# Attention scores from two float32r parts, two 64-row matmuls side by side in the array

## The chip, the cores and the metric

The kernel runs on one core of one Trainium2 chip. The metric is the device time of one execution in microseconds; the shown figure is the median of several executions. The core's engines are PE (TensorE, matrix products), DVE (VectorE), ACT (ScalarE), POOL (GpSimd) and SP (SyncE, which here only issues transfers). In the profile, PEld is the weight load of PE, which can run beside a matmul.

## The reference, cut to what matters

The input `x` is 16 batches of 512 positions of 128 numbers. Six layers are applied one after the other, each added to `x`:

```python
x = x + 0.5 * _L0_ffn_ref(_layernorm(x), ...)     # "kan"
x = x + _L0_attn_ref(_layernorm(x), ...)          # attention
x = x + 0.5 * _L0_ffn_ref(_layernorm(x), ...)     # "kan" again
x = x + 0.5 * _L1_ffn_ref(_layernorm(x), ...)     # experts
x = x + _L1_attn_ref(_layernorm(x), ...)          # a recurrence
x = x + 0.5 * _L1_ffn_ref(_layernorm(x), ...)     # experts again
```

The change lies in the attention. It has 16 query heads of 8 dimensions; 4 query heads share one key and value head; queries and keys are rotated by position (`rope`):

```python
att = jnp.einsum('bhqd,bhkd->bhqk', q, k) * scale
att = jnp.where(causal, att, jnp.finfo(att.dtype).min)
att = jax.nn.softmax(att, axis=-1)
y = jnp.einsum('bhqk,bhkd->bhqd', att, v)
```

Everything is float32.

## The kernel before, in words

**Two stages.** The attention stage goes through the 16 batches in order. Behind it the experts' stage does the three last layers. The order of the instructions on every engine is written out by hand: a batch's loop (called a row below) has 44 turns (`TURNS`), 11 banks of scores for each of the 4 key heads `r`. In each turn the main work is written down first (one bank of `weights` of batch b, one bank of `maxima` of batch b+1), and then `turn()` lets every side generator (outputs, the two kans, the projection of a later batch, the routing) write down one step, as far as the turn's budget `MOST` of each engine allows. An engine executes its instructions in that order.

**Scores twice.** A score tile of one key head and one block of 128 positions is computed twice. `maxima` (line 612) has 128 queries on the output's rows and keys along it; DVE masks it and takes the maximum over the keys (lines 617 and 622). The wider banks are masked on PE first (line 608). `weights` (line 675) has 128 keys on the rows and queries along it; ACT takes the exponential (line 678) and POOL zeroes what lies above the diagonal (line 680). The maximum of each query is subtracted within the score matmul: it is one more contraction row, against a row of ones. A head group's 11 banks hold 16 matmuls, four each of 512, 384, 256 and 128 columns, in `maxima` and in `weights` alike.

**Operands.** PE multiplies bf16 here, so that float32 queries and keys are cut into three bf16 parts (`parts`, lines 394 to 407: a copy on ACT and three subtractions on POOL, for queries and for keys), written to DRAM and read back as 9 products of parts: 72 contraction rows (`spread`, lines 477 and 485). `max_rows` cuts the maxima into three parts, turns them on PE, and brings them by way of DRAM into rows 96 to 98 of the query tile (lines 626 to 653). So `maxima` contracts over 72 rows and `weights` over 99. Ten query tiles `QP` and three key tiles `KP` go round; a query tile is read by `maxima` in one row and by `weights` in the next.

**Outputs.** `outputs` (lines 686 to 723) multiplies the weights by the values: 32 output rows for each of the 4 query heads of a group, the fourth of the array's columns for each (line 698). Eight of each 32 rows are values and one the sum. ACT copies (line 703), PE turns 4 blocks (line 711), DVE divides (lines 715 and 716), once for each `r`.

**Score banks.** PSUM has two banks for `maxima` (`scp`) and two for `weights` (`stp`).

**Experts.** Their weights are loaded at the start of the last batch's row, all at once, into query and key tiles that are free by then (lines 829 to 839).

Of the kernel before, what the change touches and what calls it, by code (L numbers as in the profile page):

```python
# [8 lines left out]
F32 = mybir.dt.float32  # L9
# [8 lines left out]
P = 128  # L18
# [11 lines left out]
NQP = 10  # L30
NKP = 3
MXR = 96
# [16 lines left out]
def tile_macaron(  # L49
# [51 lines left out]
    with ExitStack() as ph:  # L101
# [54 lines left out]
        nc.scalar.dma_start(out=gate_sb, in_=gate_in)  # L156
        rbias = cst.tile([P, 2, NV], F32, name="rbias")

        w2d = cst.tile([P, 2, NV, MH], F32, name="w2d")
        eye4 = cst.tile([P, MH], F32, name="eye4")  # L160
# [6 lines left out]
        KR = NR * HD  # L167
        wq = cst.tile([D, NH, HD], F32, name="wq")
        nc.sync.dma_start(out=wq, in_=wq_in.rearrange("k (h d) -> k h d", d=HD))
        wk = cst.tile([D, 2, NR, HD], F32, name="wk")  # L170
        nc.sync.dma_start(out=wk[:, 0, :, :], in_=wk_in.rearrange("k (h d) -> k h d", d=HD))
# [3 lines left out]
        nc.sync.dma_start(out=wo, in_=wo_in)  # L175
# [3 lines left out]
        for b in range(1, B):  # L179
            load(b)  # L180
        hh = HD // 2
        wqr = cst.tile([D, NH, HD], F32, name="wqr")
        identb = cst.tile([P, P], BF16, name="identb")
# [3 lines left out]

        QP = [qkp.tile([P, NG, S], BF16, name=f"qp{i}", tag=f"qp{i}") for i in range(NQP)]
        KP = [qkp.tile([P, NR, S], BF16, name=f"kp{i}", tag=f"kp{i}") for i in range(NKP)]
        ROWS = slice(0, MXR + 3)  # L190

        def packed(b):
            return [QP[(NR * b + r) % NQP] for r in range(NR)], KP[b % NKP]

# [199 lines left out]
        def parts(r, dst, copies, **work):  # L394

            yield from need(**work)
            copies(dst[:, 0, :], r)
            yield
            yield from need(pool=1.15)
            nc.gpsimd.tensor_tensor(dst[:, 1, :], r, dst[:, 0, :], ALU.subtract)  # L400
            yield
            yield from need(pool=1.15)
            nc.gpsimd.tensor_tensor(r, r, dst[:, 0, :], ALU.subtract)
            yield
            yield from need(pool=1.3)
            nc.gpsimd.tensor_tensor(dst[:, 2, :], r, dst[:, 1, :], ALU.subtract)
            yield

        def spread(part, heads, name):

            scr = tc.dram_tile([3, HD, heads, S], BF16, name=name)
            for i in range(3):
                nc.sync.dma_start(out=scr[i].rearrange("d h t -> h d t"), in_=part[:, i, :])
            return scr

        def attn_in(b, st):
            _, xT = yield from norm(x[b])
            ka = w1p.tile([KR, S], F32, name="rope_ka")
            kb = w1p.tile([KR, S], F32, name="rope_kb")
            ta = w1p.tile([P, S], F32, name="rope_a")  # L420
            tb = w1p.tile([P, S], F32, name="rope_b")
            qpart = w1p.tile([P, 3, S], BF16, name="qpart")
            kpart = w1p.tile([KR, 3, S], BF16, name="kpart")
# [12 lines left out]
            pk = yield from bank([2 * KR, S], F32, "ps_pk", 0.9)  # L436
            nc.tensor.matmul(pk, lhsT=wk.rearrange("k w h d -> k (w h d)"), rhs=xT, start=True, stop=True)
            later.append(lambda: nc.vector.tensor_mul(ka, pk[0:KR, :], rope[0:KR, 0, :]))
# [3 lines left out]
            take(dve=0.7)  # L442
            pv = yield from bank([P, NT, KR], F32, "ps_v", 0.9)
            for c in range(NT):
                nc.tensor.matmul(pv[:, c, :], lhsT=xT[:, bass.ts(c, P)], rhs=wv, start=True, stop=True)
            later.append(lambda: nc.vector.tensor_mul(kb, pk[KR : 2 * KR, :], rope[KR : 2 * KR, 1, :]))
            yield
            take(dve=0.7)
            freed()
            qp_steps = parts(ta, qpart, nc.scalar.copy, act=0.6)  # L450
# [3 lines left out]
            nc.gpsimd.memset(va[:, :, :, HD:32], 0.0)  # L454
            nc.gpsimd.memset(va[:, :, :, HD : HD + 1], 1.0)
            later.append(lambda: nc.vector.tensor_copy(va[:, :, :, 0:HD], pv.rearrange("p c (r d) -> p c r d", d=HD)))
            yield
            take(dve=0.3)
# [3 lines left out]
            def keys():  # L462
                yield from need(pool=1.25)
                nc.gpsimd.tensor_tensor(ka, ka, kb, ALU.add)
                yield
                yield
                yield
                yield from parts(ka, kpart, nc.scalar.copy, act=0.6)

            yield from together(qp_steps, keys())  # L470
            qp, kp = packed(b)

            ks = spread(kpart, NR, f"ks{b}")
            qs = spread(qpart, NH, f"qs{b}")
            N = 3 * HD
            for j in range(3):
                nc.sync.dma_start(
                    out=kp[j * N : (j + 1) * N, :, :],
                    in_=ks[j].rearrange("d r t -> d (r t)").unsqueeze(0).to_broadcast([3, HD, NR * S]),
                )  # L480
            for r in range(NR):
                while taken[0] < NR * b + r - NQP + 1:
                    yield
                src = qs[:, :, r * NG : (r + 1) * NG, :].rearrange("i d h t -> (i d) (h t)")
                nc.sync.dma_start(out=qp[r][0 : 3 * N, :, :],
                                  in_=src.unsqueeze(0).to_broadcast([3, N, NG * S]))
            yield

        def centered(ps, w):

            ps = ps[:, 0 : w.shape[1]]
            nc.tensor.matmul(ps, lhsT=center, rhs=w, start=True, stop=True)
            nc.vector.tensor_copy(w, ps)
# [6 lines left out]
        def cleared(pack):  # L500

            nc.vector.memset(pack[MXR - 32 : MXR, :, :], 0.0)

        def keys_cleared(i):

            cleared(KP[i])
            nc.vector.memset(KP[i][MXR : MXR + 3, :, :], 1.0)

        def prepare():
# [26 lines left out]
            centered(psc[:, 1, :], wk[:, 0, :, :].rearrange("k h d -> k (h d)"))  # L536
# [5 lines left out]
            nc.vector.tensor_copy(wk[:, 1, :, 0:hh], wk[:, 0, :, hh:HD])  # L542
            nc.vector.tensor_copy(wk[:, 1, :, hh:HD], wk[:, 0, :, 0:hh])
# [5 lines left out]
            make_identity(nc, identb)  # L549
            nc.gpsimd.memset(causal[:, 0 : S - P], 0.0)  # L550
            make_causal_mask(nc, own, NEG)
            for i in range(1, NR):
                cleared(QP[i])
                yield
            for _ in range(16):
                yield
            for i in range(NR, NQP):
                if i - NR < NKP - 1:
                    keys_cleared(i - NR + 1)
                yield  # L560
                yield
                cleared(QP[i])
                yield
                yield
# [33 lines left out]
        def maxima(b, st):  # L598
            qp, kp = packed(b)
            for half in range(2):  # L600
                maxs = w2p.tile([P, NT, NH // 2], F32, name="maxs")
                for r in (2 * half, 2 * half + 1):
                    for c, gs in BANKS:
# [3 lines left out]
                        if not alone:  # L607
                            nc.tensor.matmul(v[:, :, n - P : n], lhsT=identb,
                                             rhs=own.unsqueeze(1).to_broadcast([P, len(gs), P]),
                                             start=True, stop=False, skip_group_check=True)  # L610
# [642 lines left out]
```

## Time and profile before

| | us |
|---|---|
| median of 3 executions (range) | 1645.51 (1640.77 to 1647.1) |
| the profiled execution | 1638.15 |
| its span | 1636.4 |
| first score matmul of `maxima` starts at | 68.1 |
| first score matmul of `weights` starts at (row of batch 0) | 118.5 |
| rows of batches 3 to 8, each | 53.9 |
| rows of batches 9 to 12 | 54.9, 57.0, 55.3, 55.1 |
| rows of batches 0, 1, 2, 13, 14, 15 | 44.1, 49.6, 55.2, 48.7, 48.2, 38.5 |
| last score matmul of `weights` ends at | 948.2 |

The profiled execution's own time holds its span and 1.75 us around it. A row is counted from its first matmul on line 675 to that of the next. Durations of single instructions are given in us or ns; a matmul's duration in the profile is longer than the time in which PE can start the next one, so that what PE needs for a stream of matmuls is read from their starts.

### The profile page before, as it was taken

Reading aid. Unit: us, or ns where it says so; the run is one execution under the profiler, and the core shown is the slowest. Engines: PE = TensorE matmul, PEld = TensorE weight load, DVE = VectorE, ACT = ScalarE, POOL = GpSimd, SP = SyncE. Lnnn points to the kernel's source line nnn. Section 1 sums busy time; section 2 is a strip of 40 time slices with the busy share of each in tenths; the row PEclk is TensorE's granted clock in tenths of the full one; section 3 lists DMA queues with packets and bytes.
Section 4 is the critical chain, followed back from the end, with each engine's and each line's share of the span. In section 5 each row is a group of like instructions: output and inputs, shape, how many; then the busy total and the mean of one; then the engine's idle time right before and its main releaser. Section 6 shows DMA issues by size and latency. Waiting matters only on the chain.

```text
span 1636.4 us, 33218 instructions
## 1 busy us (share of the span) xinstructions
PE 1527.1 (93%) x11881; PEld 1062.5 (65%) x11881; DVE 1173.9 (72%) x3646; ACT 988.6 (60%) x1884; POOL 977.5 (60%) x1455
## 2 busy tenths in 40 slices
PE   5689999999999999999998899999998999999998
PEld 2234444454445444445444479999997999999998
DVE  6578878888888888888898345975579755873343
ACT  3336677877778777777766865444443444444443
POOL 2634566566655664665564666667665566756673
PEclk9779999999999999999999999999999999999999
DMA  5110110111011100110122113223322223323332
GB/s 128 64 69 24 55 54 26 42 55 53 32 40 52 57 25 36 57 47 29 42 71 69 51 44 69 59 54 72 72 68 56 66 62 72 78 51 74 67 67 58
DMA packets 99290, 92.74 MB, mean 57 GB/s; under 512 B 13245, under 2 KB 87686, under 8 KB 98886
## 3 DMA queue, kind: packets, MB, share of 16 engines
q1 hardware_dynamic: 76732, 67.72, 13.4%
q0 software_dynamic: 21584, 22.89, 7.7%
q8 instruction: 93, 1.52, 0.4%
q14 instruction: 71, 0.58, 0.1%
q10 hardware_dynamic: 810, 0.02, 0.0%
HBM read 59.07 MB, written 35.45 MB: 58 GB/s over the span
## 4 chain that ended last, share of the span: by engine, by line
PE 70%; DVE 20%; ACT 4%; issue 3%; POOL 2%; DMA 1%; SPq 0%; DVEq 0%; POOLq 0%; ACTq 0%
PE ps_h L967 12%; PE ps_y L980 12%; PE ps_av L698 7%; PE ps_st L675 6%; PE ps_sc L612 6%; DVE below L617 5%; PE acc L931 4%; PE ps_kg L366 3%; PE ps_s L339 3%; PE ps_t L319 3%; DVE ln_st L288 2%; ACT pt L678 2%; PE ps_ko L387 2%; DVE wk L801 2%; DVE tok L799 1%
## 5 line engine op out<-in xcount | busy, mean ns | idle before, releaser
L680 POOL TENSOR_SCALAR_AFFINE_SELECT pt<-pt 128x128 f32<-128x128 f32 (+2 forms) x704 | 253.2, 367 | 326.3 <-ACT pt L678 321.2
L678 ACT ACTIVATE pt<-ps_st 128x512 f32<-128x512 f32 x682 | 368.0, 563 | 94.5 <-PE ps_st L675 89.0
L617 DVE CUSTOM_DVE_ANT_0 below<-ps_sc,causal 128x512 bf16<-128x512 f32 (+1 forms) x512 | 315.2, 616 | 79.8 <-PE ps_sc L612 64.5
L870 POOL DMA_INDIRECT xg<-xnd,tokI x256 | 254.4, 994 | 86.7 <-issue 38.3
L969 ACT ACTIVATE mo<-ps_h 128x512 f32<-128x512 f32 x256 | 152.8, 597 | 228.1 <-PE ps_h L967 227.2
L967 PE MATMUL ps_h<-xin,mw 128*128 128x128 f32 x2048 | 273.8, 277 | 0.0
L980 PE MATMUL ps_y<-mw,mo 128*128 128x128 f32 x2048 | 272.0, 276 | 0.0
L612 PE MATMUL ps_sc<-kp,qp 72*128 72x512 bf16 (+3 forms) x1024 | 258.9, 304 | 12.6 <-DVE maxs L617 7.6
L675 PE MATMUL ps_st<-qp,kp 99*128 99x512 bf16 x992 | 249.9, 303 | 16.7 <-ACT pt L678 16.2
L967 PEld LDWEIGHTS ps_h<-xin,mw 128*128 128x128 f32 x2048 | 251.8, 193 | 12.8 <-issue 10.8
L980 PEld LDWEIGHTS ps_y<-mw,mo 128*128 128x128 f32 x2048 | 250.8, 193 | 0.1
L675 PEld LDWEIGHTS <-kp 99*128 99x128 bf16 x1024 | 94.4, 100 | 175.9 <-issue 158.4
L372 ACT ACTIVATE kan_h<-kan_s,rbias,kw 128x512 f32<-128x512 f32 x256 | 205.6, 812 | 4.1 <-PE ps_kg L366 4.1
L997 POOL DMA_INDIRECT sum<-mo,tokI x93 | 151.4, 1628 | 75.7 <-ACT mo L969 16.6
L698 PE MATMUL ps_av<-pt,va 128*32 128x512 f32 (+3 forms) x2048 | 165.2, 440 | 0.0
L622 DVE TENSOR_REDUCE maxs<-ps_sc 128x2 f32<-128x512 f32 (+1 forms) x192 | 130.1, 685 | 35.0 <-PE ps_sc L612 34.5
L612 PEld LDWEIGHTS <-qp 72*128 72x128 bf16 x1024 | 96.0, 99 | 80.4 <-issue 58.0
L698 PEld LDWEIGHTS ps_av<-pt,va 128*32 128x32 f32 x2048 | 53.5, 109 | 93.6 <-issue 42.5
L295 POOL TENSOR_TENSOR ln_rstd<-ln_rstd,mhalf 128x4 f32<-128x4 f32 x96 | 102.7, 1069 | 8.0
L294 POOL TENSOR_SCALAR ln_rstd<-ln_mv 128x4 f32<-128x4 f32 x96 | 22.0, 229 | 119.6 <-DVE ln_mv L292 119.4
L319 PE MATMUL ps_t<-ident,kan_x 128*128 128x128 f32 x384 | 63.5, 289 | 30.8 <-DVE kan_x L309 21.4
L986 DVE SCALAR_TENSOR_TENSOR ye<-ps_y,gainT,ye 128x128 fp32r<-128x128 f32 x83 | 28.8, 347 | 83.4 <-ACT ye L983 83.1
(196 smaller groups left out, 2487.5 us busy)
## 6 DMA issues: line engine op xcount, KB each, us to landing
qp<-qs SPq DMA_DIRECT2D x64, 288.0 KB
xnd<-kan_x SPq DMA_DIRECT2D x32, 256.0 KB
sum<-x SPq DMA_DIRECT2D x62, 128.0 KB
qs<-qpart SPq DMA_DIRECT2D x48, 128.0 KB
kp<-ks SPq DMA_DIRECT2D x48, 96.0 KB
x<-in_L_attn_x_dram SPq DMA_DIRECT2D x16, 256.0 KB
mw<-in_L_ffn_w_dram SPq DMA_DIRECT2D x16, 256.0 KB
xg<-xnd,tokI POOLq DMA_INDIRECT x256, 2.6
```

Source lines behind the costliest of these rows:

```text
L372: nc.scalar.activation(h, sk[half], AF.Relu, bias=rbias[:, half, v : v + 1], scale=kw1[:, half, v : v + 1])
L612: nc.tensor.matmul(v[:, u, 0:n], lhsT=qp[r][0 : 9 * HD, g, bass.ts(c, P)], rhs=kp[0 : 9 * HD, r, 0:n], start=alone, stop=(u == len(gs) - 1 ...
L617: nc.vector.tensor_tensor_reduce(below[:, 0:n], v[:, 0, 0:n], causal[:, S - n : S], 1.0, LOWEST, ALU.add, ALU.max, accum_out=maxs[:, c, h ...
L675: nc.tensor.matmul(v[:, u, 0:n], lhsT=kp[ROWS, r, bass.ts(c, P)], rhs=qp[r][ROWS, g, c * P : S], start=True, stop=True)
L678: nc.scalar.activation(o, v[:, :, 0:n], AF.Exp, scale=HD ** -0.5)
L680: nc.gpsimd.affine_select(out=dg, in_=dg, compare_op=ALU.is_ge, fill=0.0, base=0, pattern=[[0, len(gs)], [1, P]], channel_multiplier=-1)
L698: nc.tensor.matmul(po[32 * g : 32 * g + 32, c * P : S], lhsT=va[:, c, r, :], rhs=pt[:, g, OFF[c] : OFF[c] + n], start=(c == 0), stop=(c == ...
L870: nc.gpsimd.indirect_dma_start(out=xgs[i // E % 2][:, i % E, :], out_offset=None, in_=xnd[b], in_offset=bass.IndirectOffsetOnAxis(ap=tokI[ ...
L967: nc.tensor.matmul(pst[:, f, :], lhsT=mw1[e][:, bass.ts(f, P)], rhs=xins[i // E % 2][:, i % E, :], start=True, stop=True)
L969: nc.scalar.activation(hs[u], pst, AF.Gelu)
L980: nc.tensor.matmul(py, lhsT=hs[u][:, f, :], rhs=mw2[e][:, f, :], start=(f == 0), stop=(f == NF - 1))
L997: nc.gpsimd.indirect_dma_start(out=sums[k, b], out_offset=bass.IndirectOffsetOnAxis(ap=tokI[g][:, n : n + 1], axis=0), in_=added[b % 2 * ( ...
```

## The change

The scores are multiplied as float32r (a four-byte format that PE takes in one pass) instead of bf16. Queries and keys are cut into two parts, so that 32 contraction rows hold the four products of parts.

- A query or key tile now has two halves. Rows 0 to 63 (`UP`) serve `maxima`: 32 rows of parts, the rest zero. Rows 64 to 127 (`LOW`) serve `weights`: 32 rows of parts, two rows (96 and 97) for the maximum's parts against ones, the rest zero. The halves are loaded separately, each when its last reader is done: `feed()`, called in every turn. There are 4 query tiles and 2 key tiles, in float32.
- `weights` and `maxima` no longer write their matmuls down themselves but hand them over. `both(2, wts, mxs)` takes two turns of each in every second turn and writes the matmuls down alternately, one of `maxima` on the upper half and one of `weights` on the lower half of the array's rows; then come the readers.
- The mask's matmul in front of the wider `maxima` banks, 128 rows before, becomes two of 64 rows.
- For batch 0, whose maxima have no weights beside them, `maxima` contracts over all 128 rows.
- `parts` has one copy and one subtraction. The keys are projected into 128 rows of 128 columns instead of 32 rows of 512. `max_rows` turns one 128x128 block of float32 per half instead of four bf16 blocks, and cuts in two parts.
- `outputs` collects two head groups in one bank (the values of the odd `r` are put 16 columns further right, among zeros), and copies, turns and divides once for the two.
- The expert weights are loaded in four portions as tiles come free, the last one when all of the last batch's scores are done.

```diff
-NQP = 10
-NKP = 3
-MXR = 96
+NKP = 2
+KM = 64
+ONE = 96
...
+        ropek = cst.tile([P, 2, P], F32, name="ropek")
+        for j in range(NT):
+            for w in range(2):
+                src = rope_in[0:HD, w, bass.ts(j, P)].unsqueeze(1).to_broadcast([HD, NR, P])
+                nc.scalar.dma_start(out=ropek[j * KR : (j + 1) * KR, w, :], in_=src)
...
+        QP = [qkp.tile([P, NG, S], F32, name=f"qp{i}", tag=f"qp{i}") for i in range(NR)]
+        KP = [qkp.tile([P, NR, S], F32, name=f"kp{i}", tag=f"kp{i}") for i in range(NKP)]
+        UP, LOW = slice(0, KM), slice(KM, P)
...
-            yield from need(pool=1.15)
-            nc.gpsimd.tensor_tensor(r, r, dst[:, 0, :], ALU.subtract)
-            yield
-            yield from need(pool=1.3)
-            nc.gpsimd.tensor_tensor(dst[:, 2, :], r, dst[:, 1, :], ALU.subtract)
...
+        def feed():
...
+            while ready("km", 1, maxed, NR * NKP - NR + 1):
+                put_keys("km", 0)
+            while ready("qm", NR, maxed, NR):
+                put_queries("qm", 0)
+            while ready("kw", 1, taken, NR * NKP - NR + 1) and (pending["kw"] != 1 or maxed[0] >= NR):
+                if pending["kw"] == 1:
+                    ones_row(0)
+                put_keys("kw", KM)
+            while ready("qw", NR, taken, NR):
+                put_queries("qw", KM)
...
+        def cleared(t, eng):
+
+            eng.memset(t[KM // 2 : KM, :, :], 0.0)
+            eng.memset(t[KM:P, :, :], 0.0)
...
+                        rows = UP if b else slice(0, P)
...
+                        elif not alone:
+                            for i in range(2):
+                                runs.append((v[:, :, n - P : n], eyes[:, i, :],
+                                             owns[:, i, :].unsqueeze(1).to_broadcast([KM, len(gs), P]), i == 0, False))
                         for u, g in enumerate(gs):
+                            runs.append((v[:, u, 0:n], qp[rows, g, bass.ts(c, P)], kp[rows, r, 0:n],
+                                         alone, u == len(gs) - 1))
...
+            queue = nc.scalar if filling[0] else nc.sync
+            queue.dma_start(out=scr.rearrange("i h (c t) -> (h c) i t", c=NT), in_=mr[:, :, :].bitcast(F32))
             for k in range(2):
+                queue.dma_start(out=QP[2 * half + k][ONE : ONE + 2, :, :], in_=scr[:, k * NG : (k + 1) * NG, :])
...
+                    runs = [(v[:, u, 0:n], kp[LOW, r, bass.ts(c, P)], qp[LOW, g, c * P : S], True, True)
+                            for u, g in enumerate(gs)]
...
+        def both(times, *gs):
+
+            lanes, reads = [], []
+            for g in gs:
+                lane = []
+                for t in range(times):
+                    got = next(g, None) if g is not None else None
+                    if got is not None:
+                        lane += got[0]
+                        reads.append((t, len(lanes), got[1]))
+                lanes.append(lane)
+            for i in range(max(map(len, lanes))):
+                for lane in lanes:
+                    for out_, w, m, start, stop in lane[i : i + 1]:
+                        nc.tensor.matmul(out_, lhsT=w, rhs=m, start=start, stop=stop, skip_group_check=True)
+            for _, _, read in sorted(reads, key=lambda x: x[:2]):
+                read()
...
-        keys_cleared(0)
-        cleared(QP[0])
+        cleared(KP[0], nc.vector)
+        for i in range(NR):
+            cleared(QP[i], nc.vector if i < 2 else nc.gpsimd)
...
-                step(wts)
-                step(mxs)
+                if i % 2 == 0:
+                    both(2, wts, mxs)
```

## The prediction

> **What bounds the kernel now.** I read the page's 40 slices first. PE stands at 9 tenths from slice 4 to the end; DVE is at 7 or 8 tenths in the attention stage and lower afterwards.
>
> ```profile
> PE   5689999999999999999998899999998999999998
> DVE  6578878888888888888898345975579755873343
> ```
>
> The experts' code is untouched, so that only the first 948 us are in play. Next I took the busy times of three rows: a usual one (batch 5), the slowest (batch 10, which holds the routing), and the last, which has no maxima.
>
> ```profile
> core 0: us, PE busy (x) PEld busy (x) DVE busy (x) ACT busy (x) POOL busy (x), PEclk, DMA share, GB/s
> 375.03:428.91 53.88, 51.56 (x399) 26.22 (x399) 45.42 (x142) 42.30 (x77) 33.11 (x64) 1.00 0.14 45
> 645.51:702.46 56.95, 52.63 (x401) 26.68 (x400) 50.09 (x163) 41.14 (x76) 35.10 (x67) 1.00 0.13 42
> 909.72:948.18 38.46, 34.31 (x271) 15.62 (x268) 9.56 (x38) 31.22 (x63) 28.65 (x58) 1.00 0.18 54
> ```
>
> PE is busy for 96% of the usual row; DVE follows with 84%, ACT with 79%. The reader is to see that PE's work sets the row, and that there is little room before DVE does: in the slow row DVE reaches 88%. The matmuls of the usual row show what PE's work is:
>
> ```profile
> L675 PE MATMUL ps_st<-qp,kp 99*128 99x512 bf16 (+3 forms) x64 | 16.1, 302 | 0.9 <-ACT pt L678 0.9
> L612 PE MATMUL ps_sc<-kp,qp 72*128 72x512 bf16 (+3 forms) x64 | 15.9, 299 | 0.2
> L698 PE MATMUL ps_av<-pt,va 128*32 128x512 f32 (+3 forms) x128 | 10.3, 439 | 0.0
> ```
>
> These means overlap. What a matmul takes of PE is read from starts, in the timeline:
>
> ```profile
> 501.30 0.39 PE L675 MATMUL ps_st<-qp,kp 99*128 99x512 bf16 x1
> 501.52 0.38 PE L612 MATMUL ps_sc<-kp,qp 72*128 72x512 bf16 x1
> 501.74 0.38 PE L675 MATMUL ps_st<-qp,kp 99*128 99x512 bf16 x1
> 501.96 0.38 PE L612 MATMUL ps_sc<-kp,qp 72*128 72x512 bf16 x1
> 502.27 1.50 PE L698 MATMUL ps_av<-pt,va 128*32 128x384 f32 x24
> 503.71 0.34 PE L675 MATMUL ps_st<-qp,kp 99*128 99x384 bf16 x1
> 503.88 0.33 PE L612 MATMUL ps_sc<-kp,qp 72*128 72x384 bf16 x1
> ```
>
> A bf16 score of 512 columns takes 0.22 us, one of 384 takes 0.17; by columns, 256 take 0.11 and 128 take 0.055. From the last score to line 698, which uses a fourth of the columns, are 0.31 instead of 0.22: a change of the array's division costs 0.09.
>
> **Scores on PE.** Before: one r and one kind is 4 x (0.22 + 0.17 + 0.11 + 0.055) = 2.2 us; 8 of these are 17.8. The masks are 8 of 256 columns and 4 of 512, 1.8. Together 19.6 us a row, one after the other.
>
> After, float32r. The trace has it at 256 columns, with loads of 128:
>
> ```profile
> 974.50 0.64 PE L931 MATMUL acc<-ye 128*128 128x256 f32 x4
> 974.98 0.28 PE L931 MATMUL acc<-parts,ye 128*128 128x256 f32 x1
> 975.10 1.05 PE L967 MATMUL ps_h<-xin,mw 128*128 128x128 f32 x8
> ```
>
> Four start within 0.48 us, 0.12 each, hardly over bf16's 0.11. At 128 columns no row shows it: between 0.055 (bf16) and 0.22 (two passes of plain float32, 0.112 each on line 967). I take 0.12, the float32r row, as if the load held it. A lane is then 4 x (0.22 + 0.17 + 0.12 + 0.12) = 2.5 us per r, 10.1 per row.
>
> Do two halves of the rows run at once? No matmul pair in the trace divides rows. The nearest row divides columns: line 698.
>
> ```profile
> 502.27 0.16 PEld L698 LDWEIGHTS ps_av<-pt,va 128*32 128x32 f32 x8 [0.43 <-issue]
> ```
>
> Eight loads lie within 0.16 us though one lasts 0.106, and the 24 matmuls behind them, 0.44 on average, lie within 1.50. So parts of the array load and multiply together. Bounds for a pair: one matmul's time (10.1 us a row for both lanes) and two (20.2). I take full overlap, that row's case. The masks are now 24 matmuls of bf16, 3.5 us, on the upper half alone, written between the lower half's matmuls; I count them whole. Scores after: 13.6 us. **-6.0 per row.**
>
> [...]
>
> **Other PE work per row.** Line 711 has 16 matmuls of 0.109; half go: -0.9. `max_rows` has 8 short transposes in a division of its own (24 columns), about 0.055 each with two switches per half, 0.8; it becomes 2 of two passes at most: -0.4. The key projection (line 437, two at 0.48) becomes 16 short column-divided ones, four at once, 4 x 0.11: -0.5. Against that, 22 blocks of `both` divide the rows, and each may switch twice at 0.09; the 16 or so that the scores already pay beside lines 698, 366 and 643 stay. (44 - 20) x 0.09 = +2.1. Bounds of the switches: 0 and +4. PE's sum: -6.0 - 0.9 - 0.4 - 0.5 + 2.1 = **-5.7 us per row.**
>
> **What is late next.** DVE per row: `max_rows`' five operations, 1.7 per half in the attention stage (0.24 + 0.44 + 0.23 + 0.41 + 0.41), become two of about 0.3: -2.2. Two of 0.68 for the keys become one of 256 columns, 0.42 (as line 896): -0.9. Four divisions of 0.53 become two of about 0.68: -0.8. The values' copy splits: +0.1. Sum -3.8, to 41.6 us in the usual row. In a row of 53.9 - 5.7 = 48.2 that is 86%, below the 88% already reached. ACT loses two copies of 0.585 and half a key cast, to 40.8. POOL loses six operations of 1.15 to 1.27 and gains a wider memset, about -6; its 33 leave room anyway. So PE stays the bound in usual rows. In batches 9 to 12 DVE falls to 44 to 46, at 90% 49 to 51: they gain 5 to 5.7.
>
> Sum over rows: batches 0 and 1, 5.5 each; batches 2 to 8, 7 x 5.7 = 40; batches 9 to 12, 22; batch 13, where DVE has 44.4 of 48.7 busy, 3.5; batch 14, 5.5; batch 15, with one lane, 0.5. **-82.5.**
>
> **Start.** Three tiles are cleared on DVE ahead of the first norm, two memsets each of 1.76 (line 507's, as many elements per row): 10.6 instead of 3.6, +7. Later clears go: three of 0.91 at 21.7 to 24.7 and 7 us of them at 32 to 42, all on the chain. POOL's chain of eight operations before the first spread (43.5 to 53.8) halves: -5. The eight `ropek` issues on ACT's queue, 0.5 each, fit before its first copy at 11.8. The two or three transfers that ACT's queue issues while batch 0's maxima run wait for each other, as SP's did on line 652 (3 us each); ACT is only half busy there, and DVE sets the pace: 0, at most +6. I take -5 in all; bounds -10 and +8.
>
> **Transfers.** A row moved 4 x 288 KB of queries and now moves 8 x 256 KB; the DMA share of 0.14 leaves room. `feed()` puts them on SP's queue behind a wait for the last reader of a half, with spreads, maxima and `xnd` queued behind; each half has three r, some 35 us, until it is read. If that cover were gone the next r would wait some 3 us. The expert weights' last MB is asked for at the end of batch 15; its experts come 10 jobs later, 10 x 16 x 0.112 = 18 us, and the first slice moved 128 GB/s, 8 us for a MB. Hidden.
>
> **Sum.** -82.5 - 5 = -87.5: 1638.15 becomes 1550.6. The profiled execution is 7.4 under the median, so that the median becomes 1645.5 - 87.5 = **1558**.
>
> **Rivals.**
> 1. The halves don't overlap: PE takes each matmul of a pair in turn. Then a row's scores cost 20.2 + 3.5 = 23.7, +4.1 instead of -6.0, and a row +4.4; over 15 rows +66, less 5 at the start: **1706**. It decides from where pairs cost 1.57 times a single lane (15.8 us of 10.1), for there PE's sum is zero. For it: no row-divided pair is in the trace. Against: column-divided matmuls start 7 ns apart.
> 2. They overlap, but two banks for each kind, filled in one go, tie the engines together. PE waits at the first matmul of a block for both DVE and ACT, already 86% and 85% busy. With 0.13 us lost per block, 22 blocks are 2.9 a row, 43 in all: **1600**. For it: PE's waits for ACT and DVE at lines 675 and 612 exist (0.9 and 0.2 in the usual row). Against: they are small.
> 3. Loads of the two halves follow each other, 0.24 per pair at every width: 16 x 0.24 x 4 = 15.4, with masks 18.9, -0.7 instead of -6.0. PE per row -0.4; some 6 over the rows, 5 at the start: **1635**.
> 4. The upper bound at 128 columns, 0.22 instead of 0.12, adds 1.6 a row, 24: within the forecast's own range, **1582**.
>
> **Chances.** Forecast with case 4, 0.60 (own range 1515 to 1595); coupling, 0.14; loads in turn, 0.07, of which half within 0.5%; no overlap, 0.18; rest 0.01. A measurement of this kernel tells about 0.5%, 8 us, from no change. Faster 0.77, same 0.05, slower 0.18. Range: below, PE at its best with switches at 0 (-4 us x 14 = 56 more, cut off by DVE at half of it), 1505; above, past loads in turn, 1645. It leaves out the slower case.
>
> **What would show it.** Right: starts of lines for `weights` and `maxima` within 10 ns of each other in pairs, pairs 0.22 apart at 512 columns; rows of 48; DVE at 86%; first row no later. Wrong: pairs 0.22 apart within themselves (rival 1), PE idle in front of blocks put down to DVE or ACT (2), 0.24 per pair at 128 columns (3), transfers of queries waited for by PE.

## The result and the profile after

The changed kernel takes 1685.3 us (median of 4 executions, 1678.6 to 1689.0), the kernel before 1643.2 in the same set (4 executions, 1640.8 to 1647.1): a ratio of 1.025 with an interval of 1.021 to 1.029. The forecast was 1558, and the time lies above its range.

The profiled execution took 1678.6 us, its span is 1676.5, 40.1 more than before. Three rows of the page's 40 slices:

```profile
PE   4689989999999999999999899999998999989998
DVE  5376767778777888788777323985569755773333
PEclk9887889999999999999988799999999999999999
```

PE is as full as before. The third row is the one to read: the granted clock of PE is at 7 or 8 tenths in several slices of the attention stage (slices 2 to 6, and 21 to 23, where batches 13 to 15 are; a slice is 42 us). Before, it read 7 in slices 2 and 3 and 9 from there to the end:

```profile
PEclk9779999999999999999999999999999999999999
```

By rows (first score matmul of `weights` to that of the next row), in us; in brackets how much of it passed at half clock, added up from the trace's clock records (which begin 25.0 us into the span before and 32.0 after; they have two values, 1 and 0.5, and all but the last are 3.41 us or a multiple of it long; line 329's matmuls in the changed kernel start 0.109 us apart at 1 and 0.213 at 0.5):

| | before | after |
|---|---|---|
| start, up to the row of batch 0 | 118.5 (38.8) | 123.1 (30.7) |
| batch 0, 1, 2 | 44.0 (6), 49.5, 55.2 (3) | 51.2 (23), 52.3 (11), 61.8 (14) |
| batches 3 to 8 | 53.9 or 54.0 each (0) | 53.5 (3), 50.9, 50.9, 53.7 (7), 52.6 (3), 50.9 |
| batches 9 to 12 | 54.9, 57.0, 55.3, 55.1 (3) | 53.8, 54.8 (7), 61.1 (7), 57.8 (7) |
| batches 13, 14 | 48.7, 48.2 | 51.0 (14), 56.3 (22) |
| batches 0 to 14 | 791.3 (12.4) | 812.3 (118.4) |
| batch 15 | 38.5 (0) | 47.6 (22) |
| behind the last score | 688.2 (17) | 693.5 (16) |

So the 40 us are 21 in rows 0 to 14, 9 in the last row, 5 at the start and 5 behind the scores. A usual row (batch 5), a slow one (batch 11) and the last one, as busy time by engine:

```profile
392.73:443.58 50.85, 50.04 (x412) 27.75 (x411) 41.25 (x132) 40.02 (x75) 27.49 (x62) 1.00 0.30 74
709.31:770.40 61.09, 57.96 (x441) 30.45 (x439) 49.26 (x154) 42.40 (x78) 29.90 (x66) 0.94 0.24 63
935.44:983.07 47.63, 43.41 (x255) 21.70 (x253) 8.11 (x30) 28.34 (x56) 27.12 (x55) 0.77 0.29 86
```

The columns are span, busy PE, PEld, DVE, ACT and POOL, then the granted clock. The usual row at full clock is 3.0 us shorter than before, with PE busy for 98% of it. The last row is 9 us longer with a clock of 0.77: its PE has fewer matmuls than before (255 instead of 271), and runs at half speed for 22 us.

The groups of that usual row that answer to the three shown of before (a float32r score matmul leaves one record, each of the 64 plain float32 matmuls of line 772 two):

```profile
L753 PE MATMUL ps_sc<-kp,qp 64*128 64x512 f32 (+3 forms) x64 | 18.6, 373 | 0.3
L753 PE MATMUL ps_st<-qp,kp 64*128 64x512 f32 (+3 forms) x65 | 17.2, 361 | 0.3
L772 PE MATMUL ps_av<-pt,va 128*32 128x512 f32 (+3 forms) x128 | 10.3, 439 | 0.0
```

Busy sums of overlapping matmuls say nothing of what they cost PE. The timeline does; one block of two pairs at 512 columns:

```profile
499.61 0.61 PE L772 MATMUL ps_av<-pt,va 128*32 128x512 f32 x4
500.15 0.49 PE L753 MATMUL ps_st<-qp,kp 64*128 64x512 f32 x1
500.16 0.49 PE L753 MATMUL ps_sc<-kp,qp 64*128 64x512 f32 x1
500.49 0.39 PE L753 MATMUL ps_st<-qp,kp 64*128 64x512 f32 x1
500.49 0.39 PE L753 MATMUL ps_sc<-kp,qp 64*128 64x512 f32 x1
500.81 1.16 PE L397 MATMUL ps_ko<-wout,kan_h 128*128 128x128 f32 x8
```

The two matmuls of a pair start 3 and 4 ns apart: the halves do work side by side. But the second pair starts 0.335 us behind the first and not 0.22. The weight loads of the same block say why:

```profile
500.15 0.18 PEld L753 LDWEIGHTS ps_st<-qp,kp 64*128 64x128 f32 x1 [0.84 <-ACT kan_h L389]
500.16 0.18 PEld L753 LDWEIGHTS ps_sc<-kp,qp 64*128 64x128 f32 x1
500.26 0.19 PEld L753 LDWEIGHTS ps_st<-qp,kp 64*128 64x128 f32 x1
500.26 0.19 PEld L753 LDWEIGHTS ps_sc<-kp,qp 64*128 64x128 f32 x1
500.81 0.63 PEld L397 LDWEIGHTS ps_ko<-wout,kan_h 128*128 128x128 f32 x5 [0.36 <-issue]
```

Nothing was loaded ahead of the block: its first loads start together with its first matmuls' records, and the next ones 105 ns later. So the first pair waits some 0.105 us for its four-byte loads; the second pair's loads lie under the first pair. Behind the block the same happens to line 397: its first load starts only with its first matmul, and its second matmul follows at 501.03, 0.21 us later instead of 0.11.

The clock. Five consecutive stretches of 3.41 us in the row of batch 6, with the same columns as above (the clock is the third number from the right):

```profile
475.75:479.16 3.41, 3.41 (x25) 2.28 (x26) 1.91 (x9) 2.64 (x5) 0.78 (x3) 1.00 0.00 0
479.16:482.57 3.41, 2.89 (x24) 1.91 (x20) 3.41 (x10) 3.22 (x6) 2.58 (x4) 1.00 0.00 0
482.57:485.99 3.42, 3.42 (x13) 0.90 (x15) 2.74 (x11) 2.02 (x4) 2.55 (x6) 0.50 0.58 163
485.99:489.40 3.41, 3.41 (x29) 1.14 (x27) 1.26 (x4) 0.98 (x2) 0.59 (x2) 0.50 0.00 0
489.40:492.81 3.41, 3.41 (x29) 1.84 (x26) 2.21 (x13) 2.76 (x6) 0.59 (x2) 1.00 0.02 5
```

The clock falls behind the second stretch, in which PE is busy for 85%, and returns behind the fourth. What PE did in the second one:

```profile
479.90 0.32 PE L753 MATMUL ps_st<-qp,kp 64*128 64x128 f32 x1
480.44 0.37 PE L753 MATMUL ps_sc<-owns,eyes 64*128 64x512 bf16 x1 [0.22 <-DVE topped L669]
480.44 0.43 PE L753 MATMUL ps_st<-qp,kp 64*128 64x128 f32 x2
480.66 0.37 PE L753 MATMUL ps_sc<-owns,eyes 64*128 64x512 bf16 x1
480.68 0.41 PE L753 MATMUL ps_sc<-kp,qp 64*128 64x128 f32 x1
480.72 0.55 PE L753 MATMUL ps_st<-qp,kp 64*128 64x128 f32 x2
480.93 0.78 PE L753 MATMUL ps_sc<-kp,qp 64*128 64x128 f32 x4
481.78 0.49 PE L753 MATMUL ps_st<-qp,kp 64*128 64x512 f32 x1
482.41 0.68 PE L753 MATMUL ps_sc<-kp,qp 64*128 64x512 f32 x1
```

The halves go out of step: a 512-column matmul of one lane stands alone while the other lane waits, and 128-column matmuls, which in bf16 before started 0.055 us apart, start some 0.11 apart, as the four `ps_sc` at 480.93 do; I put that down to their loads. I gave every matmul its streaming time times the share of the array that it fills (rows/128 x columns/128), and added this up over each 3.41 us stretch of the attention stage. The streaming time is an estimate from starts in the trace of before: 0.42 ns a column at full clock, as 512 columns of bf16 started 0.215 to 0.22 us apart; twice that for a record of plain float32, whose 512 columns on line 339 took 0.431; all twice as long at half clock. In the changed kernel the 20 stretches that end in a drop have sums of 0.18 to 0.39 of the stretch; of the 193 that keep the full clock, 95% lie above 0.43, the lowest at 0.35. The 21 that end in a return lie at 0.74 to 0.94, the 21 that stay at half at 0.17 to 0.71. Streaming time alone divides them worse (drops 0.24 to 0.54, full clock kept at 0.39 to 0.90). The ranges touch: a few stretches between 0.35 and 0.39 kept the clock, and in the kernel before one of 0.30 did. Of the five stretches above, the second has 0.35, the third 0.71 and the fourth 0.88. By this reading, a fit to the traces, two halves that work one at a time count as half an idle array.

### The profile page after: what moved, and what is told of

Its sections match the earlier page's. It is cut to its first block, busy times and chain, and to the rows that moved or that the text cites. A ratio compares the mean times of both kernels' runs of the same rounds, so it can differ in the third digit from the quotient of the medians.

```text
span 1676.5 us, 33524 instructions
## 1 busy us (share of the span) xinstructions
PE 1567.9 (94%) x12061; PEld 1112.8 (66%) x12061; DVE 1120.0 (67%) x3476; ACT 955.0 (57%) x1852; POOL 905.5 (54%) x1423
## 4 chain that ended last, share of the span: by engine, by line
PE 74%; DVE 17%; ACT 4%; issue 2%; POOL 2%; DMA 0%; DVEq 0%; ACTq 0%; POOLq 0%
PE ps_h L1051 12%; PE ps_y L1064 12%; PE ps_av L772 10%; PE ps_st L753 8%; PE ps_sc L753 6%; PE acc L1015 4%; DVE below L664 4%; PE ps_kg L376 3%; PE ps_s L349 3%; PE ps_t L329 3%; DVE topped L669 2%; ACT pt L730 2%; PE ps_g L833 2%; DVE ln_st L298 2%; PE ps_ko L397 2%
## 5 line engine op out<-in xcount | busy, mean ns | idle before, releaser
L730 ACT ACTIVATE pt<-ps_st 128x512 f32<-128x512 f32 x682 | 349.0, 563 | 136.7 <-PE ps_sc L753 83.7
L753 PE MATMUL ps_sc<-kp,qp 64*128 64x384 f32 (+4 forms) x1024 | 324.0, 400 | 16.0 <-DVE topped L664 10.0
L753 PE MATMUL ps_st<-qp,kp 64*128 64x512 f32 x992 | 287.6, 382 | 15.7 <-ACT pt L730 12.9
L753 PEld LDWEIGHTS ps_st<-qp,kp 64*128 64x128 f32 x992 | 154.5, 195 | 183.8 <-ACT pt L730 82.0
L753 PEld LDWEIGHTS ps_sc<-kp,qp 64*128 64x128 f32 (+1 forms) x1024 | 171.6, 200 | 52.8 <-DVE topped L664 32.1
L772 PE MATMUL ps_av<-pt,va 128*32 128x512 f32 (+3 forms) x2048 | 187.2, 487 | 0.0
L669 DVE TENSOR_REDUCE topped<-ps_sc 128x2 f32<-128x512 f32 (+1 forms) x192 | 127.6, 684 | 21.5 <-PE ps_sc L753 18.9
L772 PEld LDWEIGHTS ps_av<-pt,va 128*32 128x32 f32 x2048 | 56.4, 115 | 81.0 <-issue 43.8
L753 PE MATMUL ps_sc<-owns,eyes 64*128 64x256 bf16 x360 | 86.6, 322 | 9.8 <-DVE topped L669 5.5
L329 PE MATMUL ps_t<-ident,kan_x 128*128 128x128 f32 x384 | 68.0, 303 | 25.6 <-DVE kan_x L319 18.2
```

The lines of the kernel that those rows point to most:

```text
L669: nc.vector.tensor_reduce(maxs[:, h : h + len(gs), c], v[:, :, 0:n], AX.X, ALU.max)
L730: nc.scalar.activation(o, v[:, :, 0:n], AF.Exp, scale=HD ** -0.5)
L753: nc.tensor.matmul(out_, lhsT=w, rhs=m, start=start, stop=stop, skip_group_check=True)
L772: nc.tensor.matmul(po[32 * g : 32 * g + 32, c * P : S], lhsT=va[:, c, r, :], rhs=pt[:, g, OFF[c] : OFF[c] + n], start=(c == 0 and not odd) ...
```

## The experiments

The theory: the overlap works and makes a row at full clock 3 us shorter; the loss is the clock, which falls because half-filled stretches stand close together, and most of the missing gain per row is four-byte loads that show at both ends of each block. Rivals: the pairs hardly overlap; or the half clock only accompanies something else that is slow (waits between engines, DMA), and costs nothing of its own. The kernels of experiments 1, 2, 4 and 5 and those of 3 and 8 ran on two other chips, on which the experts' stage took 719 to 729 us in every trace instead of 688 to 698, so they are compared by rows and by the ratio to the kernel before on the same chip. Rows are read from one trace of each kernel, and differ between traces of the same code: experiment 1 leaves batches 0 to 13 as they are, and yet batch 0 took 47.6 us there (12 at half clock) instead of 51.2 (23), batch 2 57.3 (4) instead of 61.8 (14), batch 3 56.4 (10) instead of 53.5 (3). Rows 0 to 14 took 802.7 us with 94 at half clock instead of 812.3 with 118. Rows without half clock agree within 0.1.

**1. Last row on 128 rows.** Batch 15 has no maxima beside its weights, so its matmuls can use all rows; the upper half of the key tile is cleared.

```diff
-runs = [(v[:, u, 0:n], kp[LOW, r, bass.ts(c, P)], qp[LOW, g, c * P : S], True, True)
+rows = LOW if b < B - 1 else slice(0, P)
+runs = [(v[:, u, 0:n], kp[rows, r, bass.ts(c, P)], qp[rows, g, c * P : S], True, True)
...
+if b == B - 2:
+    nc.gpsimd.memset(KP[B % NKP][UP, :, :], 0.0)
```

> Only the last batch's weights change: they contract over all 128 rows, with the keys' upper half set to zero. Theory (clock): PE's granted clock drops to half after stretches in which a small share of the array is used, and a single 64-row matmul uses half of it. Then the row of batch 15 falls from 47.6 us (22 us of it at half clock) to about 39, with under 4 us at half clock, and the total by about 8. Rival (waits: the row is long because filling two banks in one go makes PE and ACT wait for each other; the clock only follows): row 15 stays at 47 to 48 and the total within 2 us.

The ratio is 1.018 (1.011 to 1.025), an interval that overlaps that of the changed kernel, so that the row has to decide. The last row:

```profile
925.55:966.07 40.52, 35.64 (x255) 20.29 (x253) 8.09 (x30) 28.02 (x56) 26.99 (x55) 0.90 0.36 102
```

The same 255 matmuls with the same columns, the scores now on 128 rows: 40.5 us instead of 47.6, half clock 8 us instead of 22, that is 7.1 us for 14 us less at half clock. The forecast was about 39 with under 4 at half clock. This agrees with 0.5 us for each, but isn't a proof by itself: the row also has no divided blocks any more, and up to 22 switches with their exposed loads went with them.

**2. A useless matmul ahead of each block.** 128 rows, bf16, into a bank that is written anew anyway.

```diff
 lanes.append(lane)
+if lanes[0] and lanes[-1] is not lanes[0]:
+    first = lanes[0][0][0]
+    nc.tensor.matmul(first, lhsT=identb, rhs=causal[:, 0 : first.shape[1]], start=True, stop=True,
+                     skip_group_check=True)
```

> One useless bf16 matmul over the whole array (128 rows, 128 to 512 columns, overwritten by what follows) stands ahead of each block that holds weights. Its own work is 22 x 0.13 = 2.9 us a row. Theory (clock): the time at half clock in the rows of batches 0 to 14 falls from 118 us to under 40, the long rows (51 to 62 us) come near 54, rows that had full clock go from 50.9 to 54, and the total moves by less than 15 either way. Rival (waits): all rows get some 3 us longer, the total some 43.

A ratio of 1.025 (1.020 to 1.030), that of the changed kernel. The row of batch 4 grew from 50.9 to 53.8, all at full clock; 15 x 2.9 = 43.5 us of work went in. Half clock in rows 0 to 14 fell from 118 to 31 us. The sum of the rows is 812.3, as without it: 88 us less at half clock paid for 43.5 us of work, 0.5 us for each, which is what a PE at half speed loses if it has work all the time. Against the trace of experiment 1, 64 us less paid for 33.9, 0.5 again. Rows 0 and 1, in the changed kernel and here:

```profile
123.12:174.33 51.21, 47.50 (x308) 24.92 (x308) 33.75 (x98) 29.41 (x57) 21.34 (x53) 0.78 0.22 54
174.33:226.59 52.26, 48.37 (x363) 24.87 (x362) 37.91 (x119) 32.16 (x62) 24.92 (x59) 0.89 0.32 85
124.50:170.09 45.59, 42.48 (x332) 22.93 (x333) 33.82 (x98) 29.56 (x57) 21.53 (x54) 1.00 0.26 61
170.09:219.00 48.91, 46.67 (x381) 24.67 (x381) 37.93 (x118) 32.23 (x62) 24.40 (x59) 1.00 0.33 85
```

They became 5.6 and 3.4 us shorter, with no half clock left, though they have more to do. Row 0 differs by 3.6 us between the changed kernel's trace and that of experiment 1, where its code is the same, but is shorter here than in both; row 1 was 52.2 in experiment 1 too. A half clock that only accompanies another delay doesn't give that. The rows of batches 2 and 11 stayed at 61.7 and 61.6 with 10 and 3 us at half clock, so that their length isn't the clock's alone. Row 15, whose blocks got the matmul too, stayed at 47.8 with 17 us of half clock.

**3. Both, only where the clock falls.** Experiment 1, and the useless matmul in batches 0, 1 and 14 alone.

```diff
-both(2, wts, mxs)
+both(2, wts, mxs, extra=b in (0, 1, 14))
```

> Last row on 128 rows, and a useless bf16 matmul on 128 rows ahead of each block with weights in batches 0, 1 and 14 alone. Clock theory: with the extra matmul everywhere, these three rows were 5.6, 3.4 and 4.1 us shorter than in the changed kernel, and the last row on 128 rows gave 7.1; together 20 us, so that the ratio falls from 1.0249 to about 1.013, and half clock in rows 0 to 14 from 118 us to about 60. If half clock is a mere companion of something else, the sum stays within 5 us of the changed kernel's (1.022 to 1.026).

A ratio of 1.010 (1.007 to 1.013). Rows 0 and 1 are 45.6 and 48.6 (51.2 and 52.3), row 14 is 52.7 (56.3), row 15 is 40.6 (47.6); half clock in rows 0 to 14 fell from 118 to 72 us, and their sum to 798.0. Two edits, one of which only adds useless work, win back more than half of the loss (forecast 1.013). Rows 0, 1 and 14 repeat experiment 2 in a second trace.

**4. Pairs aligned.** Masks are written alone, ahead, so that each score matmul of one lane is next to one of the other.

```diff
+most = max(map(len, turns), default=0)
+for turn_ in turns:
+    turn_[:0] = [None] * (most - len(turn_))
```

> The matmuls of a block are aligned turn by turn at their ends, so that every score of the maxima stands beside one of the weights and the masks stand alone ahead of them. In the changed kernel 22 of 64 score matmuls a row had no partner. If the order is the reason, nearly all 64 start in pairs, a full-clock row falls from 50.9 by 22 x 0.13 = 3 us, and the total by 20 to 45 (less if the clock falls further because less of the array is in use). Rival (partners fall apart because the two lanes wait for different banks): pairs and rows as they were, total within 8 us.

A ratio of 1.022 (1.017 to 1.027), not clear of the changed kernel's. The full-clock row is 51.4, not shorter, and 28 of the 64 score matmuls of the weights start within 20 ns of one of the maxima (32 in the changed kernel). So the order isn't what parts the others. That the lanes wait for different banks, one for ACT, one for DVE, isn't tested by itself; the waits of the changed kernel's usual row agree (engine, line, waited for: us in total, times, longest):

```profile
PEld ps_st L753 <- ACT pt L730: 5.5, 10, 0.8
```

**5. Outputs of two groups alone,** added to the kernel before.

```diff
 (kernel before)
+the changed kernel's `outputs`, its values' tile and its rows of `wo`; rden with two buffers
```

> The kernel before with one part of the change: outputs of two head groups in one bank, one copy, four turns and one division for the two. Scores stay bf16 on the whole array, one after the other. Expected by the working: PE -0.9, ACT -1.2, DVE -0.7 us a row, rows from 53.9 to 53.0, total -13 (ratio 0.992). Rival (clock): with less PE work the clock drops in more stretches, over 40 us at half clock in the rows of batches 0 to 14 instead of 12, and the total is the same or up to 10 us longer.

A ratio of 1.000 (0.998 to 1.003). The usual row is 53.1, 0.8 us shorter, as worked out:

```profile
854.18:905.01 50.83, 46.86 (x346) 23.77 (x344) 38.38 (x127) 33.10 (x63) 18.51 (x49) 0.90 0.19 60
373.06:426.18 53.12, 50.79 (x392) 25.36 (x391) 44.02 (x139) 41.17 (x75) 32.97 (x65) 1.00 0.14 45
```

But row 14 (first line) has a clock of 0.90 and takes 50.8 instead of 48.2; half clock in rows 0 to 14 is 36 us instead of 12. Row 15 went from 38.5 to 41.0, with 10 us at half clock. The small saving was eaten where PE has pauses, even with no half-filled scores; it is one trace of each kernel.

**6. Operands of two bytes.** The scores read only the upper two bytes of each part, as bf16; that leaves out the accuracy that the lower bytes carry.

```diff
-QP[r][:, :, :].bitcast(F32R)
+QP[r][:, :, :].bitcast(BF16).rearrange("p r (s w) -> p r s w", w=2)[:, :, :, 1]
```

> The changed kernel, but its score matmuls read the upper two bytes of each float32 part as bf16 (every second two-byte element), so that loads and streams are bf16 while tiles, transfers, order and the 64-row halves stay; the scores are only bf16-accurate. Theory (loads): at the start of a block the first pair waits 0.105 us for its four-byte load, because nothing loads ahead across a change of the array's division, and at 128 columns a pair is held by its load. Then the second pair of a 512-column block starts 0.25 after the first instead of 0.335, and a full-clock row falls from 50.9 to about 48.5. Rival (the 0.105 is a fixed cost of the changed division): 0.335 stays, the row stays within 0.7 of 50.9.

A ratio of 1.005 (1.003 to 1.007), 2.0% below the changed kernel's by the ratios. One block:

```profile
497.32 0.40 PE L753 MATMUL ps_st<-qp,kp 64*128 64x512 bf16 x1
497.32 0.40 PE L753 MATMUL ps_sc<-kp,qp 64*128 64x512 bf16 x1
497.56 0.38 PE L753 MATMUL ps_st<-qp,kp 64*128 64x512 bf16 x1
497.87 0.38 PE L753 MATMUL ps_sc<-kp,qp 64*128 64x512 bf16 x1
```

The second pair comes 0.24 us behind the first instead of 0.335: the 0.1 us is the four-byte load. (The fourth matmul comes later for another reason; experiment 4 shows how the lanes part.) The forecast row of 48.5 didn't come: rows 4 and 5 still take 51.1 us, now with 3.4 us of half clock in each, which is 49.4 if that costs half.

**7. Lane after lane.** The same matmuls, written first for one lane and then for the other.

```diff
-for i in range(max(map(len, lanes))):
-    for lane in lanes:
-        for out_, w, m, start, stop in lane[i : i + 1]:
+for lane in lanes:
+    for out_, w, m, start, stop in lane:
```

> The same blocks, but all of the weights' matmuls first and then all of the maxima's, instead of alternately. Theory (the overlap is real and worth its matmuls): only the last of the one lane and the first of the other run together; per r and row 2 x 0.22 + 2 x 0.17 + 6 x 0.12 = 1.5 us more, a full-clock row 50.9 becomes 56 to 57, and half clock grows since less of the array is used at a time. Rival (waits and switches eat what the overlap gives): the row within 1.5 us of 50.9.

The span is 1694.1 us (one execution); the full-clock row is 51.9, only 1.0 longer. Taken alone that would speak for the rival, that the pairs gain little. The timeline shows that it tests nothing of the kind:

```profile
399.72 0.49 PE L752 MATMUL ps_st<-qp,kp 64*128 64x512 f32 x1
399.73 0.49 PE L752 MATMUL ps_sc<-kp,qp 64*128 64x512 f32 x1
400.06 0.39 PE L752 MATMUL ps_st<-qp,kp 64*128 64x512 f32 x1
400.06 0.39 PE L752 MATMUL ps_sc<-kp,qp 64*128 64x512 f32 x1
```

The program has both `ps_st` ahead of both `ps_sc`, and the records show them in pairs all the same: the first `ps_sc` starts at 399.73, 0.33 us ahead of the second `ps_st`, which is written before it. So what stands ahead of the prediction, that an engine executes in the order written, doesn't hold for these matmuls on different halves.

**8. The overlap by itself.** To take it away, both lanes must use the same half. The weights' operands come from a tile of zeros, once on the lower half (the control) and once on the upper one.

```diff
-runs = [(v[:, u, 0:n], kp[LOW, r, bass.ts(c, P)], qp[LOW, g, c * P : S], True, True)
+runs = [(v[:, u, 0:n], zeros[LOW, bass.ts(c, P)].bitcast(F32R), zeros[LOW, 0:n].bitcast(F32R), True, True)
...
+runs = [(v[:, u, 0:n], zeros[UP, bass.ts(c, P)].bitcast(F32R), zeros[UP, 0:n].bitcast(F32R), True, True)
```

> Control for the next run. The weights' score matmuls take both operands from a tile of zeros, on the same half (rows 64 to 127) as in the changed kernel, so that the scores behind them are all zero and the attention becomes a plain mean over the earlier positions; the number, shapes and order of the instructions are those of the changed kernel. Expected by every theory: rows at full clock as in the changed kernel, 50.9 us within 0.7, and rows 0 to 14 together 812 us within 8.

> The same zeros, read from rows 0 to 63, the half of the array on which the maxima stand; nothing else differs from the run on the lower half, so the two matmuls of a pair can't run at once. Leaves out what the control leaves out. If the overlap of the halves is worth what the starts suggest (64 pairs in 10.1 us of streaming instead of 20.2), the rows at full clock become 10 us longer, some 60 us, and the starts of a pair lie 0.22 us apart at 512 columns; as single matmuls on half the rows use half of the array, there should be more half clock as well, so rows 0 to 14 grow by 150 us or more. If the pairs gain little by lying on two halves (DVE at 41 us and ACT at 40 us would show behind them), the rows grow by less than 3 us.

One execution each: spans of 1712.7 and 1869.0, rows 0 to 14 at 817.1 and 979.7. The usual rows, control first:

```profile
508.78:561.13 52.35, 51.55 (x411) 27.80 (x410) 41.36 (x132) 40.01 (x75) 27.39 (x62) 0.97 0.25 67
```

```profile
525.49:586.90 61.41, 61.00 (x412) 35.77 (x411) 42.17 (x132) 41.02 (x75) 27.65 (x62) 0.94 0.24 61
```

The control had no usual row without half clock: 52.35 with 3.4 us of it, 50.6 if that costs half, so that the 50.9 stands. On the same half the matmuls of a block start one after the other:

```profile
525.49 0.50 PE L755 MATMUL ps_st<-zeros 64*128 64x512 f32 x1
525.83 0.39 PE L755 MATMUL ps_sc<-kp,qp 64*128 64x512 f32 x1
526.06 0.40 PE L755 MATMUL ps_st<-zeros 64*128 64x512 f32 x1
526.30 0.39 PE L755 MATMUL ps_sc<-kp,qp 64*128 64x512 f32 x1
```

1.13 us for the block (to 526.62) instead of 0.66. A row is 9.1 us longer, and rows 0 to 14 together 163, in which half clock more than doubled (130 to 294 us). The overlap is real. Of the 9.1 us, 1.7 are 3.4 us more of half clock at half a microsecond each, so that the overlap itself is worth some 7 us a row at full clock; of the 163, half are the clock's by that price. The rival is out. The fit to the clock holds here too: the drops come behind stretches with streaming up to 0.67 of the time but a share of the array of at most 0.37.

**9. Blocks of one turn.** `both(1, ...)` in every turn instead of `both(2, ...)` in every second.

```diff
-if i % 2 == 0:
-    both(2, wts, mxs)
+both(1, wts, mxs)
```

> Blocks of one turn of each kind instead of two: 44 a row instead of 22. Theory (a block costs by its entry: 0.1 us to change the division, 0.105 for the first load, 0.1 to change back): up to 22 x 0.3 = 6.6 us more, a full-clock row becomes 54 to 57. Rival (two banks filled in one go tie PE to ACT and DVE): the waits get shorter and the row falls by 1 to 2 us.

A span of 1721.2 (one execution). Usual rows take 53.2 to 54.7 instead of 50.9, for 31 runs of scores between other matmuls instead of 19 (not all of the 22 further blocks stand apart): 0.2 us for each at full clock (batch 4, 53.2), 0.3 where 3.4 us of half clock are in it. The sum of a switch (0.09) and two exposed loads (0.1 each) is somewhat more.

**10. Kernel before with outputs of two groups and a filled clock.** Experiment 5, and a useless 128-row matmul at every second bank in batches 0 and 13 to 15.

```diff
+if i % 2 == 0 and (b == 0 or b >= B - 3):
+    nc.tensor.matmul(v[:, 0, 0:n], lhsT=identb, rhs=causal[:, 0:n], start=True, stop=True)
```

> The run with the outputs part alone, and in batches 0, 13, 14 and 15, where PE isn't the bound, a useless full-array matmul ahead of every second bank of the weights (2.9 us a row). Theory (clock): in those rows the half clock goes (28 us before, under 7 now), the rows of batches 14 and 15 fall from 50.8 and 41.0 to 48.5 and 38.5, batch 0 from 45.1 to 43.5, and the total falls by 6 against that run; against the kernel before the ratio is 0.996. Rival (those rows are bound otherwise): they get 1 to 3 us longer each, ratio 1.004.

A ratio of 1.002 (1.000 to 1.003). Half clock in rows 0 to 14 went back to 14 us, but rows 14 and 15 take 51.9 and 41.0, no less than without it (50.8 and 41.0): the added work costs what the clock gives. Usual rows keep the 53.1, and the total isn't below the kernel before. No version tried here is.

## Why the prediction was wrong

By its own steps, in us of the profiled span; 40.1 more came where 87.5 less were forecast, a miss of 128.

- **Overlap of the halves** (full overlap taken, in the Scores step): right. Starts 3 to 4 ns apart, and some 7 us a row at full clock in experiment 8. But only 32 of 64 start within 20 ns of a partner, which the sum had for all.
- **Scores with their switches** (-6.0 and +2.1): -3.0 a row measured from starts (21.1 us instead of 24.1 with the masks), -3.9 forecast. (The working takes off 20 switches where its own words have 16; with 16 the forecast gain would have been 0.4 smaller. And its 120 ns "at 128 columns" is the spacing of 256-column matmuls; the changed kernel's 128-column scores start 0.11 apart, so that the 0.12 taken for them held.) The 0.335 us of a block's first pair was not in the sum: the trace of before shows loads one under the other at line 698, and I carried that over to the first load behind a change of division.
- **Other PE work** (-1.8 a row): 0.0. Line 711's half went as forecast (-0.9), and so did the key projection (-0.4, forecast -0.5); `max_rows` was -0.1 (forecast -0.4). What the sum left out ate the rest: the matmuls that were lines 319, 387 and 731 grew by 0.4, 0.3 and 0.2, those of the values and of the query projections by 0.2 each, and lines 339 and 751 by 0.1 each. On line 397 (387 before) the rows shown have the reason, a first four-byte load that shows behind a 64-row block; for the others it is taken to be the same. With PE's sum at -3.0 instead of -5.7 this is 15 x 2.7 = 40 us of the miss.
- **The step that failed**: "a row of 53.9 - 5.7 = 48.2", with the sum over rows made from it, counts all of PE's time at full clock. The rows shown of before had a clock of 1.00, and nothing in the sum asked whether half-filled matmuls and loads that show would keep it there. Half clock in rows 0 to 14 rose by 106 us and in row 15 by 22; at 0.5 us for each, as experiment 2 measured it, that is 64 us of the miss (52 with the 24 us less of experiment 1's trace). The clock records have two levels, 1 and 0.5, and steps of 3.41 us (6.83 us at half clock in the stretch shown, two steps); what stands ahead of a drop is, by the sums over such steps in the changed kernel (0.18 to 0.39) and in experiment 8 (at most 0.37), better told by the share of the array than by the time.
- **What is late next** (DVE 41.6, ACT 40.8, POOL some 27): right, 41.25, 40.02 and 27.49, and in usual rows none of them became the bound. The slow rows didn't gain: DVE has 49.3 of 61.1 us in batch 11, not the 90% that I let it set. Some 10 us of the miss are left here, of which I know only that the clock isn't all of it (61.6 us with 3 us of half clock in experiment 2). Which wait it is stays open.
- **Start** (-5): +4.7. DVE's clears were priced rightly: the first normalized tile comes at 17.55 instead of 9.92. But the later clears that go gave nothing back by batch 0's first projection, which starts at 47.75 instead of 39.02: three clears of 1.80 now stand on POOL from 30.34 to 35.84, ahead of a norm. POOL's shorter chain then did (last part of the keys ready at 55.1 instead of 53.8). The first score matmul is late again, at 76.3 instead of 68.1, 21.2 us behind that point instead of 14.3. In both kernels it starts straight behind a kan's last matmuls (line 397, started at 75.37; line 387 before, at 67.14), which waited for ACT; so the trace puts this delay to work that stands ahead of it in PE's order. The transfers of the first tiles, issued on SP's queue from 56.8 to 66.1, run beside it, and no wait for them is shown.
- **Row 15** (-0.5): +9.1, of which the clock is 11.
- **Expert weights** (hidden): 5 us are lost behind the scores. This stage varies by as much from one trace to another (693.5 to 697.9 in the changed kernel and experiments 6, 7 and 9, but 694.7 in experiment 10 too, which has the score tiles of before), so no cause is claimed.

Rival 2, engines tied by their banks, is true in kind: half of the pairs apart, and 5.5 us of waits for ACT, most of them under other work, since PE is busy for 50.0 of 50.85 us. Rival 3 is excluded by loads that start 4 ns apart, rival 1 by experiment 8. The slower side was reached by a mechanism that wasn't among the rivals.

## What to carry to other kernels

Before a change that makes PE's work smaller or half-filled, read the granted clock beside its busy time, and add up over stretches of 3.41 us, the steps of the clock records here, how much of the array streams. In the changed kernel every drop came behind a stretch below 0.4, though not every such stretch was followed by one, and the full clock came back behind stretches of 0.74 and more; these are fits to this kernel's rows, to be read again in another. Count a separate block in another division of the array as the switch and the first load on both of its sides, 0.2 to 0.3 us with four-byte operands here (experiment 9), and so make few, long blocks. A saving on PE in a row with pauses can be eaten by the clock (experiment 5: row 14 took 50.8 us instead of 48.2, at a clock of 0.90), so look whether it stays.

## What the runs showed of the hardware

- The clock fell while PE was busy: in experiment 8, whose score matmuls fill 64 of the array's 128 rows, behind stretches in which PE streamed for up to 0.67 of the time, none of them with a share of the array over 0.37. More work made rows shorter (batch 1: 52.3 to 48.9 us in experiment 2, 48.6 in experiment 3).
- Matmuls on different halves of the rows started in another order than the program's (experiment 7: a `ps_sc` at 399.73, the `ps_st` written before it at 400.06); on the same half they started one after the other, 0.23 to 0.24 us apart at 512 columns behind a block's first (experiment 8).
- Two-byte operands shortened the first pair of a block by 0.1 us (0.335 to 0.24, experiment 6). At 384 columns the four-byte operands started as close as bf16's did: 0.174 us apart in row 15, 0.17 before.
